# A megakernel's hand-written issue order exchanged for another one

## The chip, the cores and the metric

The kernel runs on one NeuronCore of one Trainium2 chip. It is a single program for two transformer blocks. The metric is the device time of one execution in microseconds (us), as the median of several runs; the profile is one execution taken by the hardware profiler.

## The reference

The batch is 16 sequences of 256 tokens with 256 features, 16 heads of 16. Block one is a cross attention with RMS norms before and after. Block two is a decoder layer: layer norm and causal self attention with rotary embedding, layer norm and cross attention to the same context, layer norm and a GELU MLP of 1024. Everything is in float32. Cut to what is computed:

```python
q_norm = rmsnorm(query, g_q); c_norm = rmsnorm(context, g_c)
Q, K, V = heads(q_norm @ Wq), heads(c_norm @ Wk), heads(c_norm @ Wv)
attn = softmax(where(mask, Q K^T * scale, -inf))
x = rmsnorm(query + (attn V) @ Wo, g_out)

h = ln(x, ln1); q, k, v = h @ sa_wq, h @ sa_wk, h @ sa_wv
x = x + attention(rope(q), rope(k), v, causal) @ sa_wo
h = ln(x, ln2); q, k, v = h @ ca_wq, y @ ca_wk, y @ ca_wv
x = x + attention(rope(q), rope(k), v) @ ca_wo
h = ln(x, ln3); x = x + gelu(h @ fc1_w + fc1_b) @ fc2_w + fc2_b
```

## The kernel before

**Tiling.** There are 48 attentions, one for each of the 16 sequences in each of the three attention layers. They are numbered 0 to 47 in the order that `ORDER` gives (its digit is the layer: 0 cross attention of block one, 1 causal, 2 cross attention of block two). While PE works on the scores and values of attention i, the projections, norms, divisions and transfers of its neighbours run in between. After the last attention the MLP follows for eight pairs of sequences (class `Mlp`).

**The order.** All engines take their instructions in the order in which the program issues them. In the attention part that order is a text, `PLAN`: a list of 2640 words. `step(word)` keeps a generator for each word; the first time a word stands in the list the function of that name runs up to its first `yield`, each later time up to the next one. So `q.9` standing eight times is eight pieces of one function in order. Instructions of a piece go to the ends of the queues of their engines (PE, DVE, ACT, POOL, and SP for most DMAs). No scheduler moves anything after that (`tc.manual_schedule()`). A DMA of `load_piece` and `load_later` goes by POOL's queue; all others here by SP's.

**The words that matter, with their lines.** `scores.i.n` (line 937): first piece 16 to 32 matmuls into two S buffers of PSUM (fp32 on line 955, or fp32r on line 966 in attentions whose `fast` is true), then two pieces of one exponential each on ACT (line 978), and for causal ones two masks on POOL (line 986). There are only two S buffers, so each score segment uses both. `values.i.n`: the product with V into the single A buffer (line 1009); in the middle and after the end (`take_last`) ACT copies it out (line 1024). `q`, `k`, `v`, `project`: 32 matmul records into one of three d buffers (lines 635 and 647), then ACT adds the bias (762), DVE rotates (770, 776, 812, 865), masks or adds. `q_high`, `q_low`, `q_out` and `k_high`, `k_low`, `k_out`: for fast attentions, split into two fp32r parts on ACT and DVE (825, 832, 836, 877, 881) and a DMA that brings them to the partitions where scores read them (842, 889). `heads_in` (1032), `sums_in` (1043): DMAs of the attention's output and sums; `invert` (1052, 1053, 1056, 1062): the reciprocal on DVE, a DMA to DRAM and one back, spread over the heads; `divide` (1067, 1069): a check sum on POOL and the multiplication on DVE; then `project` and the residual sum (1082). `stats`, `norm` (545, 555): layer norm on DVE; `turn`: transposition on PE (570) and a copy (577); `pieces`, `pieces_in` (586, 594, 600): the same by DVE and two DMAs. `send`, `receive` (719, 726): the norm factors of the queries by DRAM. `keep` (623): the output bias on POOL.

**What does not come from the text.** Before it stand the loads, `first_qk` and the first statistics; after it the MLP, written out in loops. The MLP's first steps stand in the text as `mlp.0.*` and `mlp.1.*`; `mlp.0.up2` is its first product, whose two results ACT copies at once (line 1245).

```python
    def step(word):
        if word not in steps:
            steps[word] = begin(word) or iter(())
        next(steps[word], None)
```

Of the kernel before, what the change touches and what calls it, by code (L numbers as in the profile page):

```python
# [55 lines left out]
scores.0.1 stats_x.2 values.0.0 q.1 scores.0.2 stats_y.2 v.1 scores.0.2 stats_y.2 scores.0.2  # L56
stats_x.3 values.0.1 load_piece.5.0 scores.0.3 stats_x.2 k.1 scores.0.3 stats_x.3 send.2 stats_y.3
scores.0.3 k.2 v.1 load_piece.5.1 v.1 send.2 k.1 values.0.1 send.3
scores.1.0 k_high.2 k_low.2 load_early.4 q.2 scores.1.0 send.3 scores.1.0 values.0.2 receive.2
load_early.3 scores.1.1 k_out.2 values.0.3 scores.1.1 q.3 q.2 scores.1.1 take_last.0 load_early.0  # L60
q_high.2 scores.1.2 q_low.2 values.1.0 scores.1.2 q_low.2 heads_in.0 v.2 v.2 stats_y.6 scores.1.2
q_out.2 scores.1.3 v.2 sums_in.0 k.3 stats_x.6 scores.1.3 receive.3 scores.1.3 load.4 values.1.1
k_high.3 values.1.1
scores.2.0 invert.0 values.1.2 k_low.3 scores.2.0 q.3 values.1.3 scores.2.0 heads_in.0 take_last.1
q_high.3 scores.2.1 invert.0 v.3 v.3 k_out.3 q_low.3 stats_x.6 scores.2.1 q_low.3 sums_in.1
scores.2.1 stats_y.3 values.2.0 stats_x.4 scores.2.2 stats_x.4 q_out.3 k.4 scores.2.2
load_piece.6.0 send.4 v.3 send.4 scores.2.2 load_piece.5.3 values.2.1 send.6 divide.0 k_high.4
stats_y.4 scores.2.3 invert.0 q.4 invert.1 scores.2.3 k_low.4 scores.2.3 receive.4 invert.1
stats_x.8 values.2.1
scores.3.0 heads_in.1 stats_x.8 values.2.2 scores.3.0 heads_in.1 fold_of_att load_piece.6.1  # L70
scores.3.0 q.4 load_early.2 load_later.1 values.2.3 divide.0 stats_y.4 q_high.4 invert.1
scores.3.1 send.8 take_last.2 project.0 scores.3.1 q_low.4 k_out.4 q_low.4 scores.3.1 values.3.0
project.0 fold_of_att q_out.4 scores.3.2 project.0 v.4 v.4 divide.1 scores.3.2 stats_y.8 project.0
scores.3.2 values.3.1 load_piece.5.2 finish.0 fold_of_att load_piece.7.2 scores.3.3 stats.5
values.3.1 k.6 scores.3.3 v.4 stats.5 scores.3.3 values.3.2 load_piece.7.0 sums_in.2 norm.5
k_high.6
scores.4.0 load_piece.7.1 k_low.6 values.3.3 scores.4.0 divide.1 fold_of_att turn.5 take_last.3
scores.4.0 send.6 project.1 fold_of_att turn.5 sums_in.3 invert.2 scores.4.1 heads_in.2 divide.2
project.1 load_later.0 q.5 project.1 scores.4.1 heads_in.2 fold_of_att project.1 scores.4.1
values.4.0 invert.2 invert.3 q.5 load_piece.6.2 scores.4.2 finish.1 heads_in.3 k.5 scores.4.2 q.5  # L80
q.5 load_early.1 scores.4.2 invert.3 values.4.1 q.5 receive.6 k.5 q.5 scores.4.3 k_out.6
values.4.1 q.6 k.5 q.5 q.5 invert.2 k.5 scores.4.3 v.5 v.5 stats_y.6 k.5 scores.4.3 k.5 heads_in.3
load_piece.6.3 values.4.2 q.6 stats.7
scores.5.0 q_high.6 values.4.3 stats.7 q_low.6 scores.5.0 v.6 q_low.6 scores.5.0 take_last.4
scores.5.0 q_out.6 divide.2 scores.5.0 send.8 scores.5.1 v.5 divide.3 v.6 norm.7 project.2
invert.3 scores.5.1 pieces.7 scores.5.1 pieces.7 scores.5.1 values.5.0 sums_in.4 project.2
scores.5.2 project.2 scores.5.1 k.8 v.6 scores.5.2 project.2 divide.3 pieces_in.7 scores.5.2
scores.5.2 values.5.1 finish.2 k_high.8 scores.5.2
scores.6.0 values.5.1 heads_in.4 project.3 load_later.6 stats.9 scores.6.0 load_piece.7.3 k_low.8
scores.6.0 stats.9 values.5.2 invert.4 stats_y.10 load_later.4 invert.4 scores.6.1 load_later.9  # L90
take_last.5 q.7 scores.6.1 norm.9 keep.5 pieces.9 scores.6.1 values.6.0 project.3 divide.4
# [1975 lines left out]
```

## Time and profile before

| what | value |
|---|---|
| median of 3 runs | 879.82 us (879.47 to 880.5) |
| the profiled execution, as a run | 880.08 us |
| its span, first to last instruction | 878.4 us |
| PE busy with matmuls | 867.9 us (99%) |
| DVE busy | 660.0 us (75%) |
| ACT busy | 593.4 us (68%) |
| POOL busy | 352.9 us (40%) |
| mean granted TensorE clock | 1.000 |

A page of the profile lists busy times, a row of 40 slices of the span (each digit the busy share in tenths, 9 for 90% and more), the groups of instructions by line with their mean duration and the idle time before them, and the chain of work that ended last. The ends of matmuls are modelled, so a busy PE can still be waiting; the start of a matmul is measured. "idle <-X" names what ended an idle time. Times of a timeline count from the first instruction. In a group "x16" is the number of matmul records; an fp32 matmul leaves two.

### The profile page before, as it was taken

The numbers are of one execution on the slowest core, as the hardware profiler recorded it, in microseconds if no ns is written. First come the engines' busy times: TensorE is split into PE (matmuls) and PEld (weight loads), VectorE is DVE, ScalarE is ACT, GpSimd is POOL, SyncE is SP. The second block draws the span as 40 slices with busy tenths as digits, with TensorE's granted clock in tenths as the row PEclk, the third lists the DMA queues.
The fourth block names the chain that finished last, engine by engine and source line by source line (L and its number), as shares of the span: only waits on it lengthen the run. The fifth ranks groups of instructions, "written<-read, shape, count | busy, mean of one in ns | idle before, by whom it ended". The sixth has DMA issues, their size and how long they took to land.

```text
span 878.4 us, 32887 instructions
## 1 busy us (share of the span) xinstructions
PE 867.9 (99%) x13762; PEld 558.9 (64%) x13762; DVE 660.0 (75%) x1487; ACT 593.4 (68%) x848; POOL 352.9 (40%) x558
## 2 busy tenths in 40 slices
PE   8999999999999999999999999999999999999997
PEld 4455555555555555555555555555556899999997
DVE  5368888888787878788776788888784787787562
ACT  4788767877787877788777787788876733333440
POOL 4154685257355357264555534334152132222000
PEclk9999999999999999999999999999999999999999
DMA  8576465455344345443343333224331022211201
GB/s 275 182 225 189 134 182 178 148 164 167 117 153 131 110 138 169 144 132 118 126 134 125 113 115 131 95 83 155 124 110 52 14 72 73 67 55 30 69 25 51
DMA packets 101454, 107.04 MB, mean 122 GB/s; under 512 B 26602, under 2 KB 81778, under 8 KB 101298
## 3 DMA queue, kind: packets, MB, share of 16 engines
q1 hardware_dynamic: 96210, 89.89, 31.1%
q0 software_dynamic: 4400, 14.42, 5.6%
q8 instruction: 110, 1.80, 0.9%
q10 hardware_dynamic: 688, 0.54, 0.2%
q14 instruction: 46, 0.38, 0.1%
HBM read 46.33 MB, written 13.65 MB: 68 GB/s over the span
## 4 chain that ended last, share of the span: by engine, by line
PE 86%; DVE 4%; DMA 3%; issue 2%; SPq 2%; ACT 2%; POOL 1%; ACTq 0%; DVEq 0%; POOLq 0%
PE d L647 17%; PE d L635 16%; PE A L1009 15%; PE S L966 8%; PE upX L1223 6%; PE S L955 6%; PE A L1321 6%; PE downZ L1321 3%; PE upZ L1223 3%; PE d L1321 2%; PE d L1223 2%; ACT pt L978 1%; PE d L570 1%; PE downX L1321 1%; DMA hT<-turn_hop 1%
## 5 line engine op out<-in xcount | busy, mean ns | idle before, releaser
L978 ACT ACTIVATE pt<-S 128x1024 f32<-128x1024 f32 x224 | 218.6, 1025 | 87.7 <-PE S L955 56.5
L1009 PE MATMUL A<-pt,va 128*32 128x256 f32 (+1 forms) x3072 | 183.1, 362 | 0.1
L978 ACT ACTIVATE pt<-S,sy 128x1024 f32<-128x1024 f32 x128 | 137.0, 1116 | 28.6 <-PE S L966 16.1
L1009 PEld LDWEIGHTS A<-pt,va 128*32 128x32 f32 x3072 | 94.3, 110 | 63.9 <-issue 7.4
L986 POOL TENSOR_SCALAR_AFFINE_SELECT pt<-pt 128x512 f32<-128x512 f32 x128 | 94.4, 757 | 77.3 <-ACT pt L978 76.7
L966 PEld LDWEIGHTS S<-qm,kT 32*128 32x128 f32 x1920 | 66.6, 183 | 49.6 <-issue 23.6
L966 PE MATMUL S<-qm,kT 32*128 32x256 f32 x1920 | 92.6, 303 | 1.5 <-ACT pt L978 1.3
L623 POOL TENSOR_TENSOR cur<-cur,bias 128x512 f32<-128x512 f32 x48 | 63.8, 1334 | 39.4 <-DVE xn L555 39.2
L527 POOL TENSOR_SCALAR r_ln<-bmv 128x2 f32<-128x2 f32 x48 | 15.6, 325 | 138.5 <-DVE bmv L546 137.4
L1024 ACT COPY av<-A 128x512 f32<-128x512 f32 x96 | 56.6, 590 | 20.6 <-PE A L1009 20.4
L1245 ACT COPY g<-upX 128x512 f32<-128x512 f32 x28 | 15.0, 589 | 72.4 <-issue 68.1
L955 PE MATMUL S<-qm,kT 32*64 32x512 f32 (+1 forms) x1152 | 63.5, 512 | 0.0
L635 PE MATMUL d<-hT,sa 128*32 128x256 f32 x1024 | 61.4, 381 | 0.4 <-DMA hT<-turn_hop 0.4
L762 ACT ACTIVATE a<-d,qk_bias 128x256 f32<-128x256 f32 x128 | 53.9, 477 | 4.6 <-PE d L635 4.4
L555 DVE TENSOR_SCALAR xn<-cur,bmv,r_ln 128x256 f32<-128x256 f32 x96 | 49.2, 561 | 5.3 <-POOL r_ln L528 5.3
L776 DVE TENSOR_TENSOR a<-a,turn 128x512 f32<-128x512 f32 x64 | 48.5, 758 | 1.6
L1261 ACT ACTIVATE g<-g,fb 128x256 f32<-128x256 f32 x96 | 41.0, 499 | 11.1 <-DVE g L1250 11.1
L776 DVE TENSOR_TENSOR u<-u,turn 128x512 f32<-128x512 f32 x64 | 47.8, 747 | 0.0
L770 DVE STREAM_SHUFFLE u<-a 128x512 f32<-128x512 f32 x64 | 47.4, 740 | 0.3 <-issue 0.2
L635 PEld LDWEIGHTS d<-hT,sa 128*32 128x32 f32 x1024 | 30.8, 109 | 24.0 <-issue 3.4
L1069 DVE TENSOR_TENSOR oT<-oT,inv 128x512 f32<-128x512 f32 x48 | 35.9, 749 | 11.3 <-issue 5.5
L1067 POOL TENSOR_TENSOR seen<-seen,sums 128x64 f32<-128x64 f32 x48 | 19.4, 404 | 57.2 <-DVE sums L1053 50.6
(175 smaller groups left out, 1667.7 us busy)
## 6 DMA issues: line engine op xcount, KB each, us to landing
kT<-hl SPq DMA_DIRECT2D x60, 256.0 KB
qm<-qm SPq DMA_DIRECT2D x60, 256.0 KB
oT<-av SPq DMA_DIRECT2D x192, 64.0 KB
inv<-inv_hop SPq DMA_DIRECT2D x96, 128.0 KB
turn_hop<-bits SPq DMA_DIRECT2D x33, 256.0 KB
hT<-turn_hop SPq DMA_DIRECT2D x92, 64.0 KB
out<-res SPq DMA_DIRECT2D x15, 256.0 KB
cur<-in_x POOLq DMA_DIRECT2D x11, 256.0 KB, 3.5
```

The source lines that it names most:

```text
L623: nc.gpsimd.tensor_tensor(t, t, bias_sb[:, row : row + D].unsqueeze(1).to_broadcast([P, NC, D]), ALU.add)
L635: nc.tensor.matmul(o, lhsT=w[:, k, at + t * P + j : at + t * P + j + 32], rhs=tokens, start=(k == 0), stop=(k == KC - 1), skip_group_check ...
L647: nc.tensor.matmul(ps[j : j + 32, c * D : (c + 1) * D], lhsT=some_tokens(src, k, c, j), rhs=w[:, k, at : at + D], start=(k == 0), stop=(k ...
L776: nc.vector.tensor_tensor(t, t, table.unsqueeze(1).to_broadcast([P, KC, S]), ALU.mult)
L955: nc.tensor.matmul(ps[64 * half : 64 * half + 64, 2 * m * u : 2 * m * (u + 1)] .rearrange("p (i s) -> p i s", i=2), lhsT=self.kT[r, t, at] ...
L966: nc.tensor.matmul(ps[:, at : at + m], lhsT=self.kd[r, i, t, kc * P : (kc + 1) * P].bitcast(F32R), rhs=self.qd[r, i, h, t, q0:S].bitcast(F ...
L978: nc.scalar.activation(pt[:, :, :w], ps[:, :, :w], AF.Exp, scale=scale)
L986: nc.gpsimd.affine_select(out=diag, in_=diag, compare_op=ALU.is_ge, fill=0.0, base=0, pattern=[[0, 2], [0, 2], [1, P]], channel_multiplier=-1,
L1009: nc.tensor.matmul(self.av[32 * r : 32 * r + 32, i, q0:S], lhsT=self.va[:, kc, 8 * t + 2 * r + i, :], rhs=pts[r // 2][:, r % 2, i * m : (i ...
L1024: copy(av, self.av)
L1223: nc.tensor.matmul(o if len(b.shape) == 2 else by_groups(o), lhsT=a[:, c * P : (c + 1) * P], rhs=b, start=(first and c % 2 == 0), stop=Tru ...
L1321: nc.tensor.matmul(ps[:, c, :], lhsT=a[f // 2][:, f % 2, c * P : (c + 1) * P], rhs=b[:, f, :], start=(first and c == 0 and f == 0), stop=True,
```

## The change

Only the text `PLAN` changes (297 lines become 295). Both texts hold the same 2640 words, each as often; the computation, the buffers, the loads and everything outside the text are the same. The order of the words was written anew by a planner outside the kernel, from durations taken out of more traces and with less slack added to each duration. Nearly every line differs, most by a few places; a line begins anew at each `scores.i.0`. The diff, cut to the lines with the words that are spoken of later:

```diff
...
-stats_x.3 values.0.1 load_piece.5.0 scores.0.3 stats_x.2 k.1 scores.0.3 stats_x.3 send.2 stats_y.3
-scores.0.3 k.2 v.1 load_piece.5.1 v.1 send.2 k.1 values.0.1 send.3
...
+load_piece.5.1 send.3 k.2 load_piece.5.0 k.1 load_early.0
...
-q_out.2 scores.1.3 v.2 sums_in.0 k.3 stats_x.6 scores.1.3 receive.3 scores.1.3 load.4 values.1.1
...
+load_early.3 stats_x.6 k_out.2 scores.1.1 values.0.3 scores.1.1 q.2 q.3 take_last.0 scores.1.1
...
-scores.2.0 invert.0 values.1.2 k_low.3 scores.2.0 q.3 values.1.3 scores.2.0 heads_in.0 take_last.1
-q_high.3 scores.2.1 invert.0 v.3 v.3 k_out.3 q_low.3 stats_x.6 scores.2.1 q_low.3 sums_in.1
-scores.2.1 stats_y.3 values.2.0 stats_x.4 scores.2.2 stats_x.4 q_out.3 k.4 scores.2.2
-load_piece.6.0 send.4 v.3 send.4 scores.2.2 load_piece.5.3 values.2.1 send.6 divide.0 k_high.4
-stats_y.4 scores.2.3 invert.0 q.4 invert.1 scores.2.3 k_low.4 scores.2.3 receive.4 invert.1
-stats_x.8 values.2.1
+scores.2.0 q_high.3 v.3 heads_in.0 scores.2.0 q_low.3 q_low.3 scores.2.0 values.1.2 stats_y.6
+q_out.3 k_high.3 scores.2.1 heads_in.0 k_low.3 values.1.3 scores.2.1 stats_x.4 k_out.3 v.3
+scores.2.1 take_last.1 stats_x.4 v.2 sums_in.1 scores.2.2 load_piece.6.1 send.4 k.4 stats_y.3
+scores.2.2 send.4 scores.2.2 load_piece.6.0 values.2.0 invert.0 scores.2.3 invert.1 k_high.4 q.4
+load_early.2 scores.2.3 stats_y.4 invert.1 v.3 receive.4 scores.2.3 heads_in.1 values.2.1 k_low.4
...
-scores.3.0 heads_in.1 stats_x.8 values.2.2 scores.3.0 heads_in.1 fold_of_att load_piece.6.1
-scores.3.0 q.4 load_early.2 load_later.1 values.2.3 divide.0 stats_y.4 q_high.4 invert.1
...
+scores.3.0 heads_in.1 values.2.1 stats_x.8 fold_of_att scores.3.0 q.4 k_out.4 stats_x.8 values.2.2
+scores.3.0 divide.0 values.2.3 stats_x.6 q_high.4 scores.3.1 invert.1 take_last.2 load_later.0
...
-q.5 load_early.1 scores.4.2 invert.3 values.4.1 q.5 receive.6 k.5 q.5 scores.4.3 k_out.6
...
-take_last.5 q.7 scores.6.1 norm.9 keep.5 pieces.9 scores.6.1 values.6.0 project.3 divide.4
-sums_in.5 q.7 scores.6.2 project.3 pieces.9 k.7 q.7 scores.6.2 heads_in.4 project.3 q.7 scores.6.2
...
+take_last.5 q.7 norm.9 scores.6.1 k_low.8 scores.6.1 pieces.9 values.6.0 q.7 project.3 sums_in.5
+scores.6.2 k.7 q.7 pieces.9 scores.6.2 heads_in.5 q.7 scores.6.2 values.6.1 heads_in.4 invert.5
+q.7 scores.6.3 invert.5 q.7 v.7 v.7 load_early.1 stats_y.8 k.7 invert.4 q.7 scores.6.3 k.7
...
-scores.7.0 v.7 project.4 stats_x.10 scores.7.0 pieces_in.9 q.8 scores.7.0 scores.7.0 values.6.3
...
+scores.7.0 divide.4 v.7 project.4 scores.7.0 k_out.8 q.8 stats_x.10 scores.7.0 scores.7.0
+values.6.3 q_high.8 pieces_in.9 stats_x.10 scores.7.1 divide.5 scores.7.0 heads_in.6 send.10
...
-sums_in.9 scores.10.1 q_low.11 values.10.0 norm.12 k.12 scores.10.2 pieces.13 q_low.11 keep.12
-turn.12 stats.16 q_out.11 scores.10.2 fold_of_fc1 load_piece.8.3 v.11 heads_in.9 scores.10.2
-values.10.1 divide.8 k.12 stats.16 turn.12 scores.10.3 invert.9 values.10.1 divide.8 q.12 divide.9
...
+stats.12 q_low.11 scores.10.1 values.10.0 q_low.11 invert.8 divide.8 stats.16 norm.12 k.12
+scores.10.2 q_out.11 fold_of_fc1 k.12 load_piece.8.3 scores.10.2 sums_in.9 k.12 v.11 turn.12
+scores.10.2 k.12 values.10.1 v.11 turn.12 scores.10.3 fold_of_fc1 k.12 values.10.1 heads_in.9 q.12
...
-scores.12.0 load_piece.10.1 v.12 values.11.2 scores.12.0 gain_fc1.0 stats.15 values.11.3
-scores.12.0 pieces.16 k_high.14 receive.14 scores.12.1 pieces.16 k_low.14 q.13 scores.12.1
-heads_in.10 stats.15 take_last.11 project.8 scores.12.1 keep.11 values.12.0 sums_in.11 invert.10
...
+scores.12.0 k.13 heads_in.10 k.14 k.13 scores.12.0 pieces.16 stats.15 heads_in.11 scores.12.0
+values.11.3 send.17 k_high.14 stats.15 v.12 heads_in.10 scores.12.1 k_low.14 project.6 q.13
+scores.12.1 take_last.11 norm.15 load_piece.9.2 sums_in.11 scores.12.1 pieces.15 values.12.0 q.13
...
-scores.14.0 load_piece.9.3 heads_in.12 stats_y.17 q.15 values.13.2 load_piece.11.2 scores.14.0
...
+q_low.15 load_piece.9.3 norm.19 scores.14.2 q_out.15 v.15 values.14.1 scores.14.2 finish.8 k.16
...
-q_out.20 norm.22 v.20 v.20 scores.19.0 scores.19.1 heads_in.18 v.19 load_piece.12.3 scores.19.1
-finish.14 turn.22 scores.19.0 sums_in.18 stats.26 scores.19.1 scores.19.2 divide.17 send.24 k.21
-scores.19.1 scores.19.2 v.20 scores.19.2 scores.19.2 stats_y.24 values.19.0 pieces_in.23 turn.22
...
+values.18.3 v.19 divide.17 load_piece.11.0 scores.19.1 norm.22 keep.23 q_low.20 turn.22
...
+pieces.23 heads_in.18 scores.19.2 stats.26 values.19.0 turn.22 v.20 sums_in.18
...
-scores.25.0 q.26 q.26 heads_in.24 scores.25.1 take_last.24 k.27 q.26 heads_in.23 scores.25.1
-finish.20 scores.25.1 heads_in.24 values.25.0 q.26 k.26 stats.31 scores.25.2 sums_in.24 k_high.27
...
+values.24.3 load_piece.14.2 q.26 k.26 scores.25.1 take_last.24 k.27 project.22 scores.25.1
+sums_in.24 q.26 scores.25.1 k.26 heads_in.23 values.25.0 k.26 scores.25.2 send.27 q.26 q.26 v.26
...
+k.26 scores.25.3 stats_y.27 heads_in.24 norm.31 scores.25.3 values.25.2 v.26 receive.27 divide.24
...
-values.25.3 heads_in.25 q.27 divide.24 scores.26.1 load_piece.13.3 take_last.25 q_high.27 norm.30
-scores.26.0 k.28 sums_in.25 scores.26.1 q_low.27 q_low.27 scores.26.1 scores.26.1 divide.24 v.27
-q_out.27 v.27 pieces_in.29 k.28 pieces.30 scores.26.0 scores.26.2 stats_y.27 k.28 project.24
...
+scores.26.0 keep.25 project.23 q.27 heads_in.24 stats.30 scores.26.0 load_piece.13.3 scores.26.0
+k_out.27 scores.26.0 values.25.3 q.27 stats.30 scores.26.1 take_last.25 q_high.27 divide.24
+sums_in.25 k.28 scores.26.1 q_low.27 heads_in.25 q_low.27 scores.26.1 norm.30 v.27 v.27
+scores.26.1 k.28 q_out.27 k.28 scores.26.0 scores.26.2 k.28 scores.26.1 project.24 k.28
+scores.26.2 scores.26.2 k.28 scores.26.2 values.26.0 pieces.30 scores.26.2 values.26.1 project.24
...
-scores.33.0 values.32.3 heads_in.32 k_high.34 stats_y.36 scores.33.1 take_last.32 k_low.34
-heads_in.31 scores.33.0 k.35 scores.33.1 project.30 k_out.34 norm.37 scores.33.1 scores.33.1
...
+scores.33.0 q_out.34 values.32.3 k_high.34 combine.2 scores.33.1 take_last.32 k_low.34 scores.33.0
+sums_in.32 k.35 scores.33.1 project.30 scores.33.1 scores.33.1 v.34 receive.36 k.35 k_out.34 v.34
...
-stats.40 values.36.3 k.39 keep.38 scores.37.1 take_last.36 q.38 k.39 scores.37.1 sums_in.36
-stats.40 k.39 scores.37.1 heads_in.35 k.39 values.37.0 q.38 k.39 scores.37.2 heads_in.36 norm.40
-v.38 scores.37.2 q.38 invert.35 scores.37.2 invert.36 values.37.1 q.38 invert.36 divide.36
-k_high.39 scores.37.3 q.38 values.37.1 q.39 q.38 scores.37.3 k_low.39 scores.37.3 q.38 k_out.39
-values.37.2 pieces.40 q.38 values.37.3 q.39 divide.35
...
+stats.40 values.36.3 k.39 scores.37.1 stats.40 take_last.36 q.38 k.39 scores.37.1 sums_in.36
+divide.35 k.39 scores.37.1 invert.35 k.39 values.37.0 q.38 k.39 scores.37.2 heads_in.36 norm.40
+v.38 v.38 scores.37.2 q.38 invert.36 scores.37.2 values.37.1 q.38 invert.36 k_high.39 q.38
+scores.37.3 values.37.1 q.38 q.39 scores.37.3 pieces.40 scores.37.3 q.38 pieces.40 values.37.2
+k_low.39 invert.36 q.38 v.38 q.39
...
-scores.38.0 pieces.40 q.39 invert.36 v.39 q.39 scores.38.0 q.39 scores.38.0 take_last.37
-scores.38.0 q.39 v.38 sums_in.37 keep.37 scores.38.1 v.38 q_high.39 pieces_in.40 stats.43
-project.35 v.39 scores.38.1 scores.38.0 q_low.39 scores.38.1 stats.43 values.38.0 q_low.39
-divide.36 scores.38.1 q_out.39 scores.38.2 invert.37 v.39 invert.37 scores.38.1 k.41 scores.38.2
...
+scores.38.0 heads_in.36 divide.35 q.39 values.37.3 k_out.39 scores.38.0 q.39 v.39 v.39 scores.38.0
+divide.36 q.39 scores.38.0 q.39 scores.38.0 scores.38.1 take_last.37 keep.35 q_high.39 v.39
+project.35 sums_in.37 scores.38.1 q_low.39 keep.38 pieces_in.40 scores.38.1 q_low.39 values.38.0
+scores.38.1 stats.43 scores.38.2 q_out.39 divide.36 scores.38.1 k.41 scores.38.2 invert.37
...
-k.40 divide.37 scores.39.1 q.40 q.40 scores.39.2 k.40 k_low.41 v.40 v.40 scores.39.2 take_last.38
-q.40 sums_in.38 q.40 k.40 values.39.0 scores.39.2 finish.36 heads_in.38 values.39.1 turn.43 k.40
-scores.39.3 values.39.1 k.40 q.41 scores.39.3 k.40 invert.38 scores.39.3 stats.42 invert.38
...
+scores.39.1 take_last.38 v.40 finish.36 scores.39.1 sums_in.38 k_low.41 scores.39.2 q.40
+values.39.0 divide.37 scores.39.2 values.39.1 k.40 scores.39.2 k.40 values.39.1 q.40 scores.39.3
+q.40 invert.38 q.41 k.40 invert.38 scores.39.3 k.40 scores.39.3 stats.42 values.39.2 q.41
...
-scores.46.0 q.47 k.47 values.45.2 divide.44 scores.46.0 q.47 values.45.3 scores.46.0 divide.44
-q.47 k_high.47 scores.46.1 take_last.45 project.44 q.47 scores.46.1 sums_in.45 q.47 scores.46.1
-k_low.47 values.46.0 q_high.47 k_out.47 scores.46.2 v.47 v.47 q_low.47 scores.46.2 q_low.47
-scores.46.2 mlp.0.norm q_out.47 values.46.1 scores.46.3 project.44 mlp.0.keep project.43 invert.45
-scores.46.3 invert.45 values.46.1 scores.46.3 mlp.0.turn project.43 heads_in.45 keep.45
-values.46.2 v.47 heads_in.45 mlp.0.turn
+scores.46.0 q.47 values.45.2 invert.43 scores.46.0 k.47 values.45.3 q.47 scores.46.0 take_last.45
+k_high.47 scores.46.1 q.47 sums_in.45 values.46.0 q.47 scores.46.1 q.47 v.47 v.47 mlp.0.stats
+scores.46.1 k_low.47 q_high.47 divide.43 k_out.47 scores.46.2 q_low.47 values.46.1 scores.46.2
+q_low.47 project.43 invert.45 scores.46.2 q_out.47 divide.44 divide.45 keep.43 values.46.1 v.47
+invert.45 scores.46.3 mlp.0.norm project.44 heads_in.45 scores.46.3 scores.46.3 project.43
+heads_in.45 values.46.2 mlp.1.stats invert.45
...
-scores.47.0 mlp.0.turn mlp.1.stats invert.45 scores.47.0 values.46.3 scores.47.0 take_last.46
-scores.47.1 mlp.1.stats sums_in.46 mlp.0.up2 scores.47.1 heads_in.46 scores.47.1 divide.45
-divide.45 values.47.0 mlp.0.turn scores.47.2 mlp.1.norm project.45 scores.47.2 invert.46
-scores.47.2 invert.46 values.47.1 heads_in.46 project.45 scores.47.3 mlp.0.mix values.47.1
-mlp.1.turn scores.47.3 invert.46 values.47.2 scores.47.3 mlp.1.turn mlp.1.turn values.47.3
-mlp.1.turn
+scores.47.0 mlp.0.turn scores.47.0 values.46.3 project.44 mlp.1.stats scores.47.0 mlp.0.turn
+mlp.0.turn take_last.46 scores.47.1 mlp.0.turn sums_in.46 mlp.0.up2 combine.7 scores.47.1
+divide.45 scores.47.1 mlp.0.keep mlp.1.norm values.47.0 scores.47.2 project.45 scores.47.2
+invert.46 keep.45 scores.47.2 invert.46 values.47.1 heads_in.46 scores.47.3 keep.46 values.47.1
+mlp.1.turn invert.46 scores.47.3 keep.47 values.47.2 mlp.1.turn scores.47.3 heads_in.46 mlp.1.turn
+mlp.0.mix values.47.3 project.45 mlp.1.turn
...
```

## The prediction

> **What bounds the kernel now.** I read the page's engine rows first, then the busy time by stretch, then who waits for whom.
>
> ```profile
> PE 867.9 (99%) x13762; PEld 558.9 (64%) x13762; DVE 660.0 (75%) x1487; ACT 593.4 (68%) x848; POOL 352.9 (40%) x558
> ...
> PE   8999999999999999999999999999999999999997
> ...
> PEclk9999999999999999999999999999999999999999
> ```
>
> PE is the bound, at full clock, almost without holes. By stretch (busy time of PE, PEld, DVE, ACT, POOL, then granted clock, DMA share, GB/s; the borders are where the plan's first and last matmuls start and end):
>
> ```profile
> 0.00:10.50 10.50, 8.27 (x91) 3.80 (x91) 4.09 (x16) 2.03 (x3) 3.97 (x17) 1.00 0.73 224
> 10.50:672.40 661.90, 658.64 (x12273) 369.43 (x12269) 519.27 (x1176) 511.38 (x667) 321.12 (x505) 1.00 0.44 143
> 672.40:878.40 206.00, 200.97 (x1414) 185.71 (x1410) 136.60 (x297) 79.97 (x178) 27.84 (x37) 1.00 0.15 50
> ```
>
> Only the middle stretch is ordered by the text that changes. Shown idle there is 661.9 - 658.6 = 3.3 us, but a matmul's end is modelled, so waits also hide inside busy time. I therefore laid the plan's matmul groups on the trace in order and took start-to-start distances: a dense group (q, k, v, project: 32 matmul records) takes 1.75 us when nothing holds it, a values segment 0.98, fp32r scores 0.68, fp32 scores 1.04, a transpose group 0.59. Against these PE loses some 13 us in all, 11 of them in the middle stretch and at the hand-over to the MLP; about 4 of those are tenths of a microsecond between groups of different kinds, which any order has. **So an ideal order could win about 7 us (0.8%), no more.**
>
> What the losses are is plainest at one place near the end of the plan, where the score segments scores.47.0 and scores.47.1 follow each other (timeline; columns: start, duration, engine, line):
>
> ```profile
> 657.13 0.75 PE L966 MATMUL S<-qm,kT 32*128 32x256 f32 x16
> ...
> 657.97 1.94 ACT L978 ACTIVATE pt<-S 128x1024 f32<-128x1024 f32 x2 [1.70 <-PE S L966]
> ...
> 659.39 0.39 PE L966 MATMUL S<-qm,kT 32*128 32x256 f32 x2
> ...
> 659.96 0.74 PE L966 MATMUL S<-qm,kT 32*128 32x256 f32 x14 [0.18 <-ACT pt L978]
> ```
>
> Each score segment fills both S buffers; the next may write only when the two exponentials have read them. From the end of one segment's matmuls (657.88) to the point where the next ran on (659.96) it took 2.1 us, the two exponentials and two handoffs. The order had put 1.56 us of other PE work between, so PE lost 0.56 us.
>
> **Part 1: PE work between score segments.** I summed, for each of the 175 neighbouring pairs, the PE segments that stand between in each order. Before, twelve gaps are under 2.2 us, with losses read from the trace: scores.47.1 1.56 us (lost 0.56); 0.1, 3.0, 38.1, 46.0 1.75 us (0.51, 0.46, 0.26, 0.21); 2.1, 12.1, 19.1, 25.1, 46.1 1.95 us (0.39, 0.30, 0.32, 0.32, 0.51); 36.1 and 43.1 2.0 us (0 and 0.14). Sum 3.98 us; loss is about 2.25 less the gap. After, seven are left: 2.2 with 0.98 us (only values.1.3 stands between: loss 2.25 - 0.98 = 1.27), 0.1 as it was (0.51), 39.3 and 46.1 at 1.95 (0.3 and 0.51), 36.1 and 43.1 as they were (0.14), 47.1 at 2.15 (0.1). Sum 2.83. **Part 1 is worth -1.1 us.**
>
> At the 0.98 gap a rule of the Trainium skill speaks against the change. The granted clock is 1.00 in all three stretches, and PE's longest wait shown in the plan is 0.6 us. "TensorE: Matmul & The Clock Gate" (section on HAM oscillation) says idle gaps above about 3.4 us send the array back to half rate. By the rule a stall that grew past 3.4 us would also slow what follows; by the row, my largest new stall is 1.3 us and keeps the clock. I take 0.
>
> **Part 2: steps set closer to what they wait for.** Slack here is the PE work between a step's place in the order and its user.
> - norm to turn: turn.12 goes from 0.68 us (lost 0.27) to 1.56; turn.22 from 1.75 (0.11) to 0, as turn.47 has in both, which lost 0.35. Net: -0.27 + 0.24 = 0.
> - scores.38.0 moves ahead of values.37.3, right behind q.38's last step, an ACT operation of 0.73 us that follows two exponentials. No causal segment before had under 0.98. Bounds 0 and +0.9 (0.73 and handoff); I take +0.25, as part of it runs while values.37.2 is on PE.
> - divide.24: before, heads_in.24 stands 14 us of PE work ahead of divide.24; after, 2.0 us. The transfer is oT<-av on SP's queue. Its only row on the chain:
>
> ```profile
> 143.08 5.26 DMA oT<-av
> ...
> 148.56 0.23 DVE oT L1069
> ```
>
> "DMA: Bandwidth & Descriptors" (anatomy of one DMA) gives about 2.0 us fixed plus bytes over 436 GB/s, fitted on the other descriptor path: 2.2 us for 64 KB. By the rule, issue (2 x 0.6) and landing take 3.4 us and divide waits 1.4; by the row, 6.5 us and 4.5. DVE takes its steps in order: behind divide.24 (0.7) stand both q_low.27 steps (0.70 + 0.43), for them q_out.27, placed 3.5 us after divide.24's place, and for it scores.27.0, 4.2 us later. A 1.4 us wait gives q_out.27 at 3.2: hidden. One of 4.5 us gives it at 6.3, 2.8 late; since q_out.46 managed with 3.0 us instead of 4.2 and lost nothing, 1.2 of that is covered: scores.27.0 is 1.6 us late, project.24 0.8 within it. The row may hold a queue's delay (it made the chain), so I lean to the short end: +0.3, ends 0 and +1.7.
> - pieces_in.9: SP issues 9.2 us of DMAs (counts times 0.35 to 0.6 us each) in the ten us of PE work before it, where it issued 8.3, because load_early.1 and pieces.9 now stand there too; k_out.8 stands directly in front in both. q.9 already lost 0.52 us to this transfer:
>
> ```profile
> 112.28 1.22 SPq L889 DMA_DIRECT2D kT<-hl  x2
> 113.54 2.05 SPq L600 DMA_DIRECT2D hT<-turn_hop  x4
> ```
>
> The step is one values segment later, but before it was also issued late, behind the same kT pair. Bounds 0 and +1.0; I take +0.2.
> - The weight load load_early.1 (sao) goes from 38 to 7.5 us ahead of project.5; 256 KB loads landed in 3.1 to 4.4 us on POOL's queue, so it is covered, with 3 us to spare; without cover it costs what is missing. stats_x.6 goes to the first section, 3.8 us behind its load; DVE stands still there anyway:
>
> ```profile
> DVE qa L796 <- DMA rq<-rq_hop: 9.2, 3, 4.9
> ```
>
> It fills that 4.9 us hole: 0; if the load is later than rq_hop, up to +1. k_out.34 has 4.2 us to scores.34.0 where it had 6.0; q_out.46, of the same size, had 3.0 and lost nothing: 0. Of the load_piece steps on POOL's queue, load_piece.9.3 comes closest, 4.1 us ahead of k.17 (10.7 before); its kind landed in 3.6 us in the middle, so it is on the edge: 0 to +1, I take +0.1. The others and the keep steps keep 5 us or more: 0.
>
> **Part 3: the hand-over.** At its end the new DVE order puts mlp.1.stats (8 instructions, 2.3 us) ahead of the copy of mlp.0.turn that mlp.0.up2 reads. Behind q_low.47 (done at 651.1 before) stand invert.45 0.35, divide.44 0.7, v.47 0.7, norm 2.3, project.43 0.7, mlp.1.stats 2.3, project.44 0.7, the copy 0.7: 8.5 us, done at 659.6; up2 started at 660.63 before, of which 0.56 was the loss of scores.47.1 and 0.2 that of scores.46.0. It is on the edge: 0 to +1, I take +0.2. In both orders ACT copies up2's two banks before scores.47.1's exponentials, so scores.47.2 and project.45 lose their 1.6 us again. mlp.0.mix and project.45's add end the plan on DVE, so the sum after the first up product frees its bank 0.3 us later: +0.2.
>
> **Sum:** -1.1 + 0 + 0.25 + 0.3 + 0.2 + 0.1 + 0.2 + 0.2 = +0.15 us. Beside the profiled span of 878.4 (880.08 us as a run, 1.7 us outside the span) that is 878.55; the median of the runs is 879.82, so **880.0 us**. What a measurement of this kernel tells from no change is about 0.2%, 1.76 us: 878.06 to 881.58.
>
> **Rivals.**
> - *Faster, 877.2 us (879.8 - 1.1 - 1.5).* Part 1 pays its 1.1, nothing in parts 2 and 3 bites, and another 1.5 of the 7 us goes because queued work shrinks: adding up DVE's and ACT's own durations along the order, DVE's longest pile-up falls from 3.3 us (q.47) to 2.6 and ACT's from 3.6 (k_high.47) to 3.2. For it: fewer short gaps. Against: most steps that this sum calls 1 to 2 us late before cost PE nothing.
> - *Slower, 882.2 us: the hand-over.* By the same sum DVE enters the stretch with 2.5 us queued at q.47, and mlp.0.turn's copy ends 2.0 us behind up2's place; up2's copies hold ACT, scores.47.2 follows, the MLP starts late: 880.0 - 0.2 + 2.0 + 0.4. It decides once the copy ends 1.8 us late. For it: DVE's order. Against: from the trace's own 651.1 the copy is just in time.
> - *Slower, 882.2 us: late DMAs hold DVE.* divide.24 by the row and q.9 at its upper end: 880.0 - 0.5 + 2.7. For it: the 5.26 us row. Against: project.23 has 3.4 us between its heads_in and divide in both orders and lost nothing.
> - *No effect:* the same losses at other places; this is the forecast's own case.
>
> **Chances.** Forecast 0.40 (878.1 to 881.5), faster 0.26, hand-over 0.18, late DMAs and waits I did not find 0.16. Hence faster 0.26, same 0.40, slower 0.34. The range leaves out one in ten on each side: 876.8 (three of the seven us won) and 884.2 (both slow cases together: 2.2 each, less 0.2).
>
> **What would show it.** Right: scores.2.2 delays k.4 by over 1 us; no loss behind scores.12.1, 19.1, 25.1, 3.0; PE idle of the plan's stretch still near 3 us; project and DVE waits on DMA under 1 us. Wrong: DVE waiting on oT<-av or inv<-inv_hop for over 1.5 us, scores.27.0 waiting for qm, mlp.0.up2 waiting for mT, or a granted clock below full.

## The result: slower by 0.7%

The changed kernel takes 886.38 us (883.30 to 890.08), the kernel before 879.97 (879.47 to 880.50); the ratio is 1.0073, 95% interval 1.0047 to 1.0098. The forecast was 880.0, in effect no change, with a range to 884.2; the measured time lies outside it. Two things are to be explained: 6.4 us, and a scatter of 7 us where the kernel before scatters by 1. The profiled execution is the longest, 890.08 us with a span of 888.4, 10.0 more than before.

The page (engine rows; the span in 40 slices) and the three stretches, again cut where the plan's first and last matmuls start and end:

```profile
PE 870.7 (98%) x13762; PEld 559.5 (63%) x13762; DVE 664.6 (75%) x1487; ACT 593.1 (67%) x848; POOL 351.4 (40%) x558
...
PE   8999989989999999999999999999999999999997
...
PEclk9999999998999999999999999999999999999999
```

```profile
0.00:10.24 10.24, 7.52 (x85) 3.48 (x85) 4.06 (x16) 2.03 (x3) 3.60 (x17) 1.00 0.74 230
10.24:682.40 672.16, 662.28 (x12273) 370.39 (x12269) 523.27 (x1175) 511.14 (x667) 319.87 (x505) 0.99 0.43 140
682.40:888.40 206.00, 200.89 (x1410) 185.65 (x1410) 137.31 (x299) 79.98 (x178) 27.93 (x37) 0.99 0.16 50
```

The opening and the MLP are as before (206.00 us in both); the middle stretch went from 661.9 to 672.2. Its PE busy time grew too, by 3.6 us with the same instructions, and the clock row has an 8: part of the loss is matmuls that run slower. Two slices of the PE row after the first have an 8. The list of waits (total, times, longest) names what stands in them:

```profile
PE S L953 <- ACT pt L976: 2.6, 1, 2.6
...
PE d L645 <- DVE oT L1067: 2.4, 1, 2.4
```

The longest wait in the plan before was 0.6 us:

```profile
PE S L966 <- ACT pt L978: 1.3, 3, 0.6
```

Around the two new ones, by stretch (columns as in the prediction; the clock is the third number from the end):

```profile
111.00:114.41 3.41, 1.14 (x20) 0.23 (x16) 1.05 (x1) 1.94 (x2) 0.65 (x1) 1.00 0.62 214
114.41:117.82 3.41, 3.27 (x32) 1.58 (x36) 2.66 (x8) 1.05 (x1) 1.14 (x2) 0.50 0.53 164
117.82:123.00 5.18, 5.18 (x112) 2.83 (x108) 3.19 (x6) 2.42 (x3) 3.26 (x6) 1.00 0.52 176
...
196.33:199.74 3.41, 1.15 (x24) 0.41 (x15) 3.37 (x5) 1.35 (x2) 1.40 (x2) 1.00 0.68 225
199.74:203.16 3.42, 3.09 (x20) 0.81 (x24) 2.98 (x7) 2.26 (x4) 0.00 (x0) 0.50 0.09 24
203.16:206.57 3.41, 3.41 (x36) 1.58 (x32) 0.00 (x0) 1.81 (x2) 2.30 (x4) 0.50 0.52 184
206.57:212.00 5.43, 5.43 (x112) 2.52 (x104) 3.52 (x8) 3.37 (x5) 2.29 (x4) 1.00 0.22 72
```

In each case PE stands still for 2.3 us of a 3.41 us stretch, and then the granted clock is 0.50 for 3.41 and 6.83 us: project.4 took 3.52 us instead of 1.93. Start to start, against the prediction's base durations, project.4 is 2.5 us late and the next group 1.6; scores.13.0 is 2.7 late and the two groups behind it 1.8 and 1.7. Unrounded that is 10.2 us, about the whole difference of the two profiled executions; the order's other gains and losses nearly cancel in this one.

**What made project.4 late** (timeline, 107 to 115 us; start, duration):

```profile
106.88 0.45 SPq L416 DMA_DIRECT2D sao<-in_sa_wo  x1
...
107.38 1.34 SPq L1060 DMA_DIRECT2D inv<-inv_hop  x2
...
113.36 1.14 DVE L1067 TENSOR_TENSOR oT<-oT,inv 128x512 f32<-128x512 f32 x1 [3.66 <-DMA inv<-inv_hop]
...
114.56 3.52 PE L645 MATMUL d<-w0o,oT 128*32 128x256 f32 x32 [2.42 <-DVE oT L1067]
```

In the kernel before the same two steps stood here, with no wait in front of the division:

```profile
104.61 1.34 SPq L1062 DMA_DIRECT2D inv<-inv_hop  x2
...
110.43 0.69 DVE L1069 TENSOR_TENSOR oT<-oT,inv 128x512 f32<-128x512 f32 x1
```

The new order sets three steps on SP's queue ahead of invert.4's last transfers (`inv`) that stood behind them or elsewhere before: the first pair of heads_in.5, invert.5's transfer to DRAM and the weight load load_early.1. SP issued `inv` at 104.61 before and at 107.38 now, and DVE waits 3.66 us for it.

**What made scores.13.0 late** (timeline, 192 to 203 us):

```profile
191.99 3.31 DVE L774 TENSOR_TENSOR a<-a,turn 128x512 f32<-128x512 f32 x1
...
192.37 1.29 POOL L621 TENSOR_TENSOR cur<-cur,bias 128x512 f32<-128x512 f32 x1
...
193.63 2.86 POOL L517 TENSOR_SCALAR fc<-fc,vec 128x1024 f32<-128x1024 f32 x1
...
195.93 2.36 DVE L810 TENSOR_TENSOR a<-a,u 128x512 f32<-128x512 f32 x1
...
196.46 1.27 POOL L621 TENSOR_TENSOR cur<-cur,bias 128x512 f32<-128x512 f32 x1
...
198.39 0.72 ACT L818 ACTIVATE qm<-a,vec 128x512 f32<-128x512 f32 x1 [4.53 <-DVE a L810]
...
200.07 2.92 PE L953 MATMUL S<-qm,kT 32*64 32x512 f32 x16 [2.59 <-ACT pt L976]
```

Of q.14's three DVE products the first and the last take 3.31 and 2.36 us; before, the three took 0.69, 0.68 and 0.69, the first of them here:

```profile
188.97 0.69 DVE L776 TENSOR_TENSOR a<-a,turn 128x512 f32<-128x512 f32 x1
```

Beside them GpSimd now runs keep.11, gain_fc1.0 and keep.12 one after the other. ACT stands behind q_high.14 for 4.5 us, so the exponentials of scores.12.3, next in ACT's order, come late, and scores.13.0 can't have its banks.

**Theory:** these two places and the half clock behind them make the loss. **Rivals:** many small losses; waits alone, with the clock no matter; the prediction's own divide.24.

### The profile page after: what moved, and what is told of

The parts are those of the page before. It is cut to its first block, busy times and chain, and to the rows that moved or that the text cites. A ratio compares the mean times of both kernels' runs of the same rounds, so it can differ in the third digit from the quotient of the medians.

```text
span 888.4 us, 32879 instructions
## 1 busy us (share of the span) xinstructions
PE 870.7 (98%) x13762; PEld 559.5 (63%) x13762; DVE 664.6 (75%) x1487; ACT 593.1 (67%) x848; POOL 351.4 (40%) x558
## 4 chain that ended last, share of the span: by engine, by line
PE 87%; DVE 4%; DMA 2%; POOL 2%; ACT 1%; issue 1%; SPq 1%; ACTq 0%; DVEq 0%; POOLq 0%
PE d L633 17%; PE d L645 17%; PE A L1007 15%; PE S L964 8%; PE S L953 6%; PE upX L1221 6%; PE A L1319 6%; PE downZ L1319 3%; PE upZ L1221 3%; PE d L1319 2%; PE d L1221 2%; PE d L568 1%; ACT pt L976 1%; PE downX L1319 1%; DMA oT<-av 1%
## 5 line engine op out<-in xcount | busy, mean ns | idle before, releaser
L984 POOL TENSOR_SCALAR_AFFINE_SELECT pt<-pt 128x512 f32<-128x512 f32 x128 | 91.0, 731 | 86.9 <-ACT pt L976 86.5
L553 DVE TENSOR_SCALAR xn<-cur,bmv,r_ln 128x256 f32<-128x256 f32 x96 | 51.6, 585 | 6.4 <-POOL r_ln L526 6.4
```

The lines of the kernel that those rows point to most:

```text
L984: nc.gpsimd.affine_select(out=diag, in_=diag, compare_op=ALU.is_ge, fill=0.0, base=0, pattern=[[0, 2], [0, 2], [1, P]], channel_multiplier=-1,
```

## The experiments

Labels are those of the runs; plan lines in the diffs are cut to the words that move.

**e1_gain, e2_inv, e3_both: steps at the two places moved back, alone and together.** e2_inv is not quite the first order: it sets invert.4's last transfers ahead of heads_in.4's second pair too, where the first order had them behind it.

```diff
 e1_gain
- scores.12.3 gain_fc1.0 values.12.2
+ scores.12.0 gain_fc1.0 pieces.16
 e2_inv
- scores.6.2 heads_in.5 q.7 scores.6.2 values.6.1 heads_in.4
- v.7 v.7 load_early.1 stats_y.8 k.7 invert.4 q.7 scores.6.3
+ scores.6.1 load_early.1 k_low.8
+ scores.6.2 q.7 scores.6.2 invert.4 values.6.1 heads_in.4
+ v.7 v.7 stats_y.8 k.7 q.7 heads_in.5 scores.6.3
```

> Changed kernel with one step, gain_fc1.0 (GpSimd, 2.9 us), moved back 12 us of PE work to just behind scores.12.0, about where the first order had it. Theory (two waits and the half clock behind each): the DVE products of q.14 take 0.69 us again instead of 3.31 and 2.36, the 2.6 us wait of scores.13.0 goes, and so does the 6.8 us at half clock behind it; the stretch 190 to 212 us loses under 1 us instead of 6.1; the stall at project.4 (111 to 118 us) stays. Median 882.5 to 884.5 against 886.4. Rival (many small losses all over the order): 885.5 or more. Rival (q.14 is late for another reason than GpSimd): the wait stays, 886.

> Changed kernel with SP's order around attention 4 and 5 as the first order had it: invert.4's transfers ahead of heads_in.5's first pair, and the weight load load_early.1 (256 KB) 9 us earlier. Theory: divide.4 no longer waits 3.7 us for inv, project.4 no longer waits 2.4 us, and the 3.4 us at half clock from 114.4 us go; the stall at scores.13.0 stays. Median 882.5 to 885 against 886.4. Rival (the DMA is late for its landing, not its place): project.4 still waits over 1.5 us and the time stays at 886.

> Both moves together. Theory: no granted clock below full ahead of the last 5 us, no PE wait over 1.2 us in the plan's stretch, median 879.5 to 881 and the runs within 1.5 us of each other instead of 7. Rival (small losses all over): 883 or more, with the spread still there.

Measured: 883.34, 885.03 and 883.75 us (ratios 1.0037, 1.0055, 1.0046; intervals of 0.0013 each way). e2_inv removed the wait of project.4 from its profile, and the drop with it. e1_gain reduced the other one: scores.13.0 was 1.1 us late and the next group 0.9. In e3_both the product still took five times its 0.69 us:

```profile
188.78 3.46 DVE L774 TENSOR_TENSOR a<-a,turn 128x512 f32<-128x512 f32 x1
...
189.15 2.53 POOL L621 TENSOR_TENSOR cur<-cur,bias 128x512 f32<-128x512 f32 x2
```

It ends at 192.24, 0.56 us after the second add (191.68). keep.11 and keep.12, which e3_both leaves, are part of the cause. The profile of e3_both had full clock until its last 2 us and a span of 880.1, but its other executions reached 885; so my 879.5 to 881 was wrong. The changed kernel's own ratio is known to 0.0025 each way, some 2 us, so these three runs do not tell the single effects apart.

**e5_keep: GpSimd's two adds moved as well.**

```diff
 e3_both and
- v.13 keep.11 q.14
- scores.13.0 keep.12 q_low.14
+ pieces.15 keep.11 values.12.0
+ q_out.11 keep.12 fold_of_fc1
```

> The two moves of e3_both, and keep.11 and keep.12 (GpSimd adds of 1.28 us) put back to where the first order had them, so that no GpSimd step over 1 us stands beside q.14's DVE products. Theory (GpSimd holds back DVE): in e3_both the first product still took 3.46 us beside the two adds and scores.13.0 came 2.0 us late; now it takes 0.69, that loss goes, and the time falls by 1.5 to 2.2 us below e3_both in a profile (span 878 to 878.6). Rival (the product is slow for its own reason): 3.46 us and the 2.0 us stay.

Measured: 880.39 us, ratio 1.0003 (0.9994 to 1.0013), span 878.6. The product is back at its length and scores.13.0 in time:

```profile
189.25 0.69 DVE L774 TENSOR_TENSOR a<-a,turn 128x512 f32<-128x512 f32 x1
```

With six steps moved, the changed order is level with the first.

**e4_busy, e6_busy20: the waits left, PE kept busy in them.** The extra matmuls write banks that are overwritten or not read.

```diff
+    def busy(ps, n):
+        for m in range(n):
+            j = 32 * (m % 4)
+            nc.tensor.matmul(ps[j : j + 32, 0:D], lhsT=w0_sb[:, 0, j : j + 32],
+                             rhs=w0_sb[:, 0, 0:D], start=True, stop=True,
+                             skip_group_check=True)
...
-            res = by_token(self.oT, self.w_o, 0)
+            res = by_token(self.oT, self.w_o, 0, 40 if self.i == 4 else 0)
...
+            if (self.i, n) == (13, 0):
+                busy(dense_ps(), 40)
```

> Changed kernel, order untouched; PE gets 40 extra matmuls of 0.055 us (2.2 us) ahead of project.4 and 40 ahead of scores.13.0, whose results are overwritten or unread, so that PE is busy where it waited. Theory (the wait itself costs 2.4 and 2.6 us and then half clock costs 1.6 and 3.5 us more): the two stages still come 2 to 2.6 us late, but the granted clock stays at 1.00 and the stages behind them take their full-rate 1.9 us; median 881.5 to 884. Rival (only the waits cost, the clock is no matter): 886 or more, as 4.4 us of work came on.

> As e4_busy with 20 extra matmuls at each of the two places, which is 2.2 us (e4_busy's 40 took 4.5 us each, twice what was meant, as one fp32 matmul is two records). Theory (waits cost 2.4 and 2.6 us, half clock 1.6 and 3.5 more): full clock behind both, the same lateness at both places; median 881.5 to 884 against 886.4. Rival (clock no matter): 886 to 890.

Measured: 890.41 us with 40 matmuls; they took 4.5 us each time, twice what was meant, so this tells only that the clock stayed full. With 20, 885.17 us; the gain over 886.38 is 1.2 us, not the 2.4 or more expected, and as the two intervals overlap (1.0040 to 1.0066 against 1.0047 to 1.0098), the medians do not settle the clock's share. The traces settle it at the two places. With the extra matmuls project.4 and scores.13.0 come 2.2 and 2.7 us late, nearly as in the changed kernel, but at full clock:

```profile
114.23 1.91 PE L654 MATMUL d<-w0o,oT 128*32 128x256 f32 x32
...
200.05 1.93 PE L633 MATMUL d<-yT,ca 128*32 128x256 f32 x32
```

In the changed kernel these two groups took 3.52 and 3.64 us. Start to start the half clock added 1.6 us behind project.4, and 0.9 and 1.7 behind scores.13.0 (where another 0.9 comes at full clock as well): 4.2 of the profiled execution's 10. By the mean granted clocks (0.993 to 0.999 over the changed kernel's executions, 0.996 on average, against 0.999 here) it is some 2.5 us in the mean, an estimate. It is not what makes every execution long: one at 0.999 still took 886.25. The profiled execution of e6_busy20, its longest (887.59), showed something else:

```profile
384.12 0.93 DVE L1078 TENSOR_TENSOR oT<-oT,inv 128x512 f32<-128x512 f32 x1 [4.09 <-DMA oT<-av]
...
390.07 1.10 PE L975 MATMUL S<-qm,kT 32*128 32x256 f32 x16 [1.73 <-issue]
```

```profile
387.56:390.97 3.41, 1.63 (x40) 1.06 (x32) 3.27 (x8) 0.58 (x1) 0.06 (x1) 1.00 0.40 156
390.97:394.39 3.42, 3.42 (x40) 1.58 (x36) 3.35 (x11) 2.12 (x2) 0.09 (x1) 0.50 0.32 115
```

This is divide.24: DVE waited 4.1 us for its transfer, scores.27.0 followed 1.8 late, and the clock fell. In the changed kernel's own profile divide.24 waited 2.01 us and PE nothing.

**e9_heads, e10_before_heads: divide.24 alone.**

```diff
 e9_heads: e5_keep and
- stats_y.27 heads_in.24 norm.31
- q.27 heads_in.24 stats.30
+ scores.25.1 heads_in.24 take_last.24
+ heads_in.23 heads_in.24 values.25.0
 e10_before_heads: the kernel before and
- q.26 heads_in.24 scores.25.1
- scores.25.1 heads_in.24 values.25.0
- scores.26.1 divide.24 v.27
+ k.26 heads_in.24 scores.25.3
+ q.27 heads_in.24 norm.31
+ q_high.27 divide.24 norm.30
```

> e5_keep with both steps of heads_in.24 put back to where the first order had them, 14 us of PE work ahead of divide.24. Theory (divide.24's late transfer is what makes some executions 3 us longer: it waited 0, 1.5, 1.6, 2.0 and 4.1 us in the profiles so far, and with 4.1 scores.27.0 came 1.7 us late and the clock halved): median 880.2 as e5_keep, but no execution above 881.5, where e5_keep had 3 of 14 at 882.3 to 883.5. Rival (the long executions come from elsewhere, as in the kernel before): one in five still above 882.

> The kernel before, with heads_in.24 and divide.24 alone set as the changed order has them (2 us of PE work apart). Theory: divide.24 waits 1.5 to 4 us for its transfer; where it waits under 2.5 nothing comes of it, where it waits 4 scores.27.0 is 1.7 us late and the clock may halve behind it: median 880 to 881, a fifth or more of the executions at 882 to 884. Rival (hidden in any case): 880 as before, with the spread of before.

Measured: 880.44 us (878.16 to 884.22) and 880.27 (879.64 to 883.90), both level with the kernel before. The theory fell: without the late heads_in.24 a third of e9_heads' executions still took over 882, and with it the first order had one long execution in fourteen. divide.24 can cost 3 us, as shown above, but it did so in one profile only.

**e7_before_late: GpSimd's three steps moved in the first order.**

```diff
 the kernel before and
- scores.12.1 keep.11 values.12.0
- scores.12.0 gain_fc1.0 stats.15
- q_low.11 keep.12 turn.12
+ norm.15 keep.11 q.14
+ pieces.15 gain_fc1.0 values.12.2
+ scores.13.0 keep.12 scores.13.0
```

> The kernel before, with keep.11, gain_fc1.0 and keep.12 alone moved to where the changed order has them. Theory: q.14's first product is held for 2 us or more by GpSimd, scores.13.0 comes 2 to 3 us late, and in executions where that wait falls in one of the clock's 3.4 us windows the clock halves for 3.4 or 6.8 us: median 882 to 886 against 880, and a spread of over 3 us. Rival (these steps alone do nothing): 880.

Measured: 880.25 us, ratio 1.0000: the rival, so moving these three words alone does no harm. In its trace keep.11 has ended and gain_fc1.0 begun when q.14's first product starts, which takes 1.08 us; keep.12 runs 7 us after that, as GpSimd first waits for another step. The place in the text does not settle what meets what; the whole GpSimd order does. The profiled execution was a long one (885.82), with no POOL step in it:

```profile
62.77 0.69 DVE L796 TENSOR_TENSOR qa<-d,rq 128x512 f32<-128x512 f32 x1 [6.30 <-DMA rq<-rq_hop]
...
64.11 1.93 PE L647 MATMUL d<-w0o,oT 128*32 128x256 f32 x32 [3.09 <-DVE oT L1069]
```

A transfer of the opening holds DVE 6.3 us and PE 3.1. Up to here the text is that of the kernel before, whose profile has 3.1 us and 0 for the same two: the transfer came 3 us later in this execution, and why is not seen.

**e8_all, e11_all: the small stalls removed too.** The first two lines name the PE segments alone.

```diff
 e8_all: e5_keep and
- scores.2.0 v.3 values.1.2 scores.2.1 values.1.3 scores.2.2 k.4 values.2.0 scores.2.3 q.4 values.2.1
+ scores.2.0 values.1.2 values.1.3 scores.2.1 v.3 values.2.0 scores.2.2 k.4 values.2.1 scores.2.3 q.4
- scores.29.1 take_last.28 q.30
+ k_low.30 take_last.28 v.30
- q_low.15 load_piece.9.3 norm.19
+ receive.17 load_piece.9.3 gain_fc1.1
- norm.22 keep.23 q_low.20
+ scores.19.0 keep.23 q_high.20
 e11_all: e8_all, heads_in.24 as in e9_heads, and
- scores.2.1 take_last.1 stats_x.4
+ v.3 take_last.1 scores.2.1
```

> e5_keep, and four small moves more in the changed order: v.3 and values.2.0, 2.1 between the scores of attention 2 as the first order had them, take_last.28 ahead of the exponentials of scores.29.1, load_piece.9.3 ahead of gain_fc1.1, keep.23 ahead of q_high.20 instead of beside norm.22. Theory (each of these was a stall of 0.7 to 1.0 us): 3 us below e5_keep in a profile, span 875 to 876, median 876.5 to 878.5, faster than both kernels. Rival (they hide one another or come back elsewhere): within 1 us of e5_keep.

> e8_all with heads_in.24 put back as in e9_heads and take_last.1 ahead of the exponentials of scores.2.1. Theory: the 1.0 us at values.2.0 that e8_all still lost to that copy goes; median 877 to 878, no execution above 879. Rival (noise of this size hides it): 878.4 as e8_all.

Measured: 878.35 us (ratio 0.9977, 0.9967 to 0.9987), then **876.35** (0.9955, 0.9942 to 0.9968), with executions from 875.97 to 877.06. e11_all beats both kernels. Its middle stretch, at full clock:

```profile
10.40:668.60 658.20, 656.66 (x12273) 368.89 (x12269) 521.89 (x1175) 510.69 (x667) 318.32 (x506) 1.00 0.45 143
```

The stretch is 3.7 us shorter than in the kernel before. Apart from heads_in.24, the moves undid stalls of 0.7 to 1.3 us: scores.2.2, values.29.0 (its accumulator bank was freed by take_last.28, which ACT had behind two exponentials), k.17, norm.22, which took 2.15 us beside keep.23's add, and values.2.0, which had come up in e8_all.

**e13_sp, e14_pool, e15_sao: each place put back into the quiet order.**

```diff
 e13_sp: e11_all without e2_inv's moves
 e14_pool: e11_all without e1_gain's and e5_keep's moves
 e15_sao: e11_all, and of e2_inv's moves only load_early.1's undone
```

> e11_all with SP's order around attention 4 and 5 as the changed order has it (load_early.1 and heads_in.5's first pair ahead of invert.4's transfers). Theory: project.4 waits 1.6 to 2.4 us for divide.4, and in some executions the clock halves behind it: 1.6 to 4 us above e11_all's 876.4, so 878 to 880.5, with a wider spread. Rival (the loss is made up at the next wait): under 877.

> e11_all with gain_fc1.0, keep.11 and keep.12 as the changed order has them. Theory: q.14's DVE products are held back, scores.13.0 comes 2.6 us late and the group behind it 0.9 us, and the clock halves behind it in part of the executions: 3 to 7 us above e11_all, so 879.5 to 883.5. Rival (as with the kernel before, where the same three moves cost nothing): 876.4.

> e11_all with load_early.1 alone (256 KB, one SP issue of 0.45 us) as the changed order has it, heads_in.5 and invert.4 as in the first order. If the weight load is what holds inv back (its bytes in the queue ahead of inv's): 1 us or more above e11_all. If it is the two transfer pairs set ahead of invert.4: under 0.5 us above e11_all, 876.4 to 876.9, and project.4 does not wait.

Measured: 878.94 us (0.9982, 0.9974 to 0.9990), 881.43 (1.0006, 0.9995 to 1.0017) and 877.12 (0.9958, 0.9949 to 0.9967). Against e11_all's 876.35, SP's order costs 2.6 us and the three GpSimd steps 5.1 (2.4 and 4.5 by the ratios, which allow for the kernel before coming out 0.4 us higher in these rounds; each is known to about 1.5). The weight load alone costs 0.8 (0.3 by the ratio), not clear of nothing. So the late `inv` is mostly due to the other transfers that e2_inv's moves had set behind it, the pairs of heads_in.5 and heads_in.4 and invert.5's transfer to DRAM; these were not separated. The clock is the smaller part of the 5.1: e14_pool's six executions at a mean clock of 1.000 have a median of 880.55, its seven others (0.996 to 0.998) 881.46. Its profile shows the wait and then the clock, on the same pattern as the changed kernel:

```profile
PE S L953 <- ACT pt L976: 2.6, 1, 2.6
```

```profile
192.74:196.16 3.42, 0.82 (x14) 0.32 (x8) 3.38 (x6) 1.88 (x3) 0.89 (x1) 1.00 0.58 185
196.16:199.57 3.41, 3.41 (x24) 0.72 (x25) 2.46 (x5) 2.26 (x3) 0.00 (x0) 0.50 0.04 5
```

e13_sp's shows the wait of project.4 with the clock still full:

```profile
PE d L645 <- DVE oT L1067: 1.5, 1, 1.5
```

The many-small-losses rival explains 4 us (e5_keep to e11_all), but not the 6.4: e5_keep still has these losses and is level with the first order, which must lose as much at other places.

**e12_stalls: waits made on purpose in the kernel before.**

```diff
+        mm(w0_sb[:, 0, 0:32], w0_sb[:, 0, 0:256], 256)
+        for _ in range(6):
+            nc.scalar.copy(held, ps[:, 0:64])
+        mm(held[:, 0:32], held, 64)
...
+            if self.i in range(10, 42, 4):
+                hold(dense_ps())
```

> The kernel before, with PE made to wait on purpose ahead of eight projects (attention 10, 14, ... 38): four matmuls, six ACT copies of them (about 1.2 us and what ACT has queued), four matmuls that read the copy; 1.5 to 4 us of PE idle each, at eight places in the clock's 3.4 us windows. Theory (half clock follows where about 2.0 us or more of a window is idle, not only after 3.4 us): behind some of the eight the granted clock is 0.50 for 3.4 us, behind the shorter ones it is 1.00; 880 plus 8 x 2 to 3 us and 1.7 us for each drop: 896 to 912. Rival (only gaps above 3.4 us drop the clock): no granted clock below full behind gaps under 3.4 us.

Measured: 900.76 us (897.82 to 902.08). ACT had little queued at these places, so the waits came out nearly alike (total, times, longest):

```profile
PE d L646 <- ACT held L652: 12.9, 8, 1.9
```

In the profiled execution none of the eight dropped the clock, though seven lay wholly within one 3.41 us window. Of the other three executions two had a mean clock of 0.997 and 0.998; they were not profiled. The waits I had wanted, over 2 us, were not reached: it shows only that shorter ones can be harmless.

## Why the prediction was wrong, step by step

- **Part 2, the sum over moved steps, failed: it costed a moved step for its own user and seldom for what stands behind or beside it.** load_early.1 was "covered, with 3 us to spare", which is true of project.5. At pieces_in.9 the prediction did count what SP issues ahead of it, but it did not follow invert.4's transfers, which now stand behind load_early.1, heads_in.5 and invert.5's transfer: 2.6 us (e13_sp).
- **gain_fc1.0, keep.11 and keep.12 do not occur in the prediction, apart from "the keep steps keep 5 us or more: 0".** They meet their own users in time. What they cost is DVE's time beside them: 5.1 us (e14_pool), the largest single term. "SBUF — State Buffer" of the Trainium skill (section on two separate sides) has the rule: a DVE instruction with two SBUF inputs and a GpSimd instruction that reads SBUF share a port pair, which the one that starts first locks for the whole instruction. The lengths beside the adds fit a lock (3.46 us, ending 0.56 after the second add, against 0.69 alone), but not who should have it: by its shown start the product began first, at 188.78 against 189.15. gain_fc1.0 fits less: a product of 0.68 us ran inside its shown span of 2.86, and GpSimd's spans are rough. So that GpSimd's steps hold the products is shown by moving them; by what means is not. In the kernel before keep.11 stood beside a small step of DVE (line 1052, 1.26 us where it takes 0.2 elsewhere), and PE lost nothing.
- **Part 1's clock step, "my largest new stall is 1.3 us and keeps the clock", failed in its first half.** The stall at scores.2.2 was sized rightly (1.3 us measured, 1.27 predicted) and did keep the clock. But two stalls of 2.4 and 2.6 us came that part 2 had not found, and the rule weighed there, gaps above some 3.4 us ("TensorE: Matmul & The Clock Gate", section on HAM oscillation), is too lax for this trace: both dropped the clock. By that rule the two places would have cost the profiled execution 6 us; by the rows they cost 10.2.
- **Right, by size or nearly:** scores.2.2, and the score gaps of 12.1, 19.1, 25.1 and 3.0, which lost nothing, so that part 1's gain did come there; the hand-over, where mlp.0.up2 did not wait; load_piece.9.3 at its upper end (k.17 0.86 late, "on the edge: 0 to +1"); load_early.1 for its own user.
- **Mis-sized:** divide.24's wait, 2.0 us in this profile against "1.4" by the rule and "4.5" by the row; the profiles have 0.8 to 4.1, and what follows at 4.1 (scores.27.0 1.8 late) is what the row's working gave (1.6). turn.22, which was to lose 0.35 like turn.47, lost 0.70, as norm.22 ran long beside keep.23. scores.38.0, forecast at +0.25, lost nothing. values.29.0 (0.95), waiting for take_last.28, was not in the list.
- **The rivals:** none was the case. "Late DMAs hold DVE" had the right kind of cause at the wrong place, divide.24 instead of divide.4. The hand-over rival and the faster case fell; part 1's 1.1 us cannot be seen in the time beside this.
- **What would have shown it:** the list named "a granted clock below full" and a DVE wait on `inv<-inv_hop` above 1.5 us as signs of error, and both came.

What stays open: why single executions of most of these orders come out 2 to 5 us long, often at full clock (the kernel before, over all its executions, ran from 878.7 to 885.3), and so part of the changed kernel's scatter of 7 us. Three such executions were profiled (e6_busy20, e7_before_late, e15_sao), and each showed another transfer late; whether that is all of it was not tried.

## What to carry to other kernels

When a step moves in a hand-written order, cost it for everything behind it on its queue and for what runs beside it, not only for its own reader: here a transfer's successors and GpSimd's neighbours on DVE made the loss, and with both moved back it was gone (e5_keep). Read the granted clock behind every PE wait over 1.5 us: a wait of 2.4 us cost 4.1 with the clock behind it (project.4), and the same wait can drop the clock in one run and not in the next. Put effects to the test in an order without other stalls: in the changed order, whose executions scatter by 7 us, moving steps back one place at a time gave no clear answer; in the quiet one each place stood out.

## What the runs showed of the hardware

- **The clock is decided in windows of 3.41 us that do not start with the wait.** In the changed kernel's clock records the drops begin at 114.41 and 199.74 us, 25 windows of 3.413 us apart, and last one and two windows. The wait of 2.6 us at scores.13.0 lay mostly within one window in the changed kernel (2.3 us idle) and in e14_pool (2.6), and the clock fell; in e2_inv a wait of the same length was split (1.1 and 1.5), and it did not. The 3.1 us of e7_before_late were split too (1.7 and 1.4) and kept the clock.
- **How much idle time within a window drops it is bounded, not found.** By the idle time that the profile shows, every window behind the opening with 2.3 us or more was followed by half clock, as far as the records reach, those at the end of the executions included. Below that the cases mix: 1.8 us (e6_busy20) and 1.6 (e15_sao) dropped it, 1.9 (e12_stalls) and 1.7 (e7_before_late) did not. As the ends of matmuls are modelled, some tenths are uncertain.
- **GpSimd's adds of 128x512 can hold a DVE product for longer than they run:** 3.46 us beside two adds (2.53 together), 2.36 beside one and the end of a tensor_scalar.
- **The same transfer lands up to 3 us later from execution to execution:** up to attention 10, e7_before_late and the kernel before have the same text, and DVE waited 6.3 and 3.1 us for the same rq<-rq_hop. Over orders with its step unchanged DVE waited 0.8, 0.8, 1.4, 1.5, 1.6, 2.0, 2.0 and 4.1 us for oT<-av at divide.24 (the 0 that I gave for one of them ahead of e9_heads was 0.8); there the work before it differs too.
